# Rounding by integer conversion and a separate stream for W_down in a cross-attention and ternary-FFN kernel

## The chip, the cores and the metric

The kernel runs on one core of one Trainium2 chip. Times are device microseconds of one execution of the program; the profile counts in microseconds from the first instruction of the profiled execution.

## The reference

There are 32 blocks of x and of the context, each 128 by 512 in f32. The first half is a cross-attention that treats the 128 rows as channels and the 512 columns as time; the second half is a feed-forward part with 8-bit activations and ternary weights. Cut to what matters:

```python
# x, ctx: (32, 128, 512); Wq, Wk, Wv, Wo: (128, 128); w_gate, w_up: (2048, 512); w_down: (512, 2048)
def xattn(x, c):                                  # 8 heads of 16 channels, rotary on the first 8
    q, k, v = Wq @ x + bq, Wk @ c + bk, Wv @ c + bv
    q, k = rope(q), rope(k)
    p = softmax(q.T @ k / 4)                      # 512 x 512 for each head
    return Wo @ (p @ v) + bo

def act_quant(x):                                 # per row
    scale = 128 / clip(max(abs(x)), 1e-5)
    return clip(round(x * scale), -128, 127) / scale

def weight_quant(w):                              # one scale for the matrix
    scale = 1 / clip(mean(abs(w)), 1e-5)
    return clip(round(w * scale), -1, 1) / scale

def ffn(x):
    g = act_quant(x) @ weight_quant(w_gate).T
    u = act_quant(x) @ weight_quant(w_up).T
    h = fwht(silu(g) * u)                         # normalized Walsh-Hadamard transform over 2048
    return act_quant(h) @ weight_quant(w_down).T

x = x + xattn(layernorm(x), ctx)
x = x + ffn(layernorm(x))
```

## The kernel before

**One stream per step.** The body of the program is some forty Python generators, one for each step of the work (`s_load`, `s_a`, ... `s_dn`), each looping over the 32 blocks (or 64 half blocks of four heads). A step yields what it needs next: an engine with an estimated duration, a buffer from a ring (`get`, given back with `p.put`), or a mark that another step sets (`on`, set with `p.mark`). The class `Plan` runs all of them against an estimated clock while the program is built, and so fixes the order of every engine's instructions, and of the DMAs on the SyncE queue (SP), which issues all DMAs. Among the steps that could start within a small window on an engine, `rank` prefers the lowest number: a constant for the step from `CFG`, plus `T` times the block, less a bonus (`stick`) for a matmul in the mode that TensorE is in. If a step names several engines, the first is preferred by `pen` microseconds, except in the last blocks. An operation that is marked `port` is planned so that VectorE's does not overlap one of GpSimd (POOL). The engines then run their instructions in that order, each waiting on semaphores.

**Attention.** `s_load` brings x and context; `s_a`, `s_a2` and `s_a3` do the layer norm, the q and k projections and the rotary part (four operations on POOL, L575 to L585) and write the result to DRAM (`xd`); `s_st` reads it back in the layout for scores. `s_mpe` computes scores only to find their row maxima on VectorE (L642, L657; `pS` is a single buffer of two banks), `s_epe` computes them again transposed with the maximum subtracted (L712, `pT`, single too), `s_eact` takes the exponential on ScalarE (L725), `s_eav` multiplies with v (L746). Score matmuls use 48 or 50 rows of the array, the v product 32 columns. `s_o` divides, projects and adds x.

**FFN.** `s_o2` normalizes, scales and rounds a block's rows to integers in bf16 (`xq`) and transposes them by DMA (L864). `s_gpe` and `s_upe` are the gate and up matmuls (L880). `s_bf` does the first four of the Hadamard's steps as adds and subtracts on POOL (L964), `s_zt` to `s_yv` the rest by transposes and matmuls. `s_am` finds the row maximum, `s_q` multiplies by the scale (L1099, POOL), `s_q1` and `s_q2` round and clip on ScalarE, and `s_dn` does the 16 down matmuls (L1141), multiplies and adds the residual on VectorE (L1147), and stores.

**Rounding.** Adding 12582912 (`MAGIC`) to an f32 number leaves its nearest integer in the low bits. x is rounded so into a PSUM buffer (L854) and brought back by VectorE (L857). y is rounded in place (L1109); L1123 then writes `relu(MAGIC + 127 - y)`, that is 127 minus the clipped integer, in bf16. So the down product has the wrong sign and an offset of 127 times W_down's column sums. One more matmul per block (L1142, two rows: `NEG` times `CS`) takes the offset out, and the sign goes into the factor `yc` (L1090).

**Weights.** W_gate, W_up and W_down (4 MB each) come as twelve pieces of 128 by 2048 into the buffers that z and y use later: `s_w` loads (L354), `s_w1` sums absolute values on ScalarE (L367) and makes the scale, `s_w2` scales and adds MAGIC (L391, ScalarE first), `s_w3` clips (L401, VectorE first), `s_w4` subtracts MAGIC into the fp8 weights (L409, ScalarE), and at the end sums W_down's columns for `CS` (L418, 16 matmuls, four small VectorE operations and a DMA). Block 0's gate matmuls wait for all three matrices:

```python
            if b == 0:
                yield "on", "wr", 2
```

Of the kernel before, what the change touches and what calls it, by code (L numbers as in the profile page):

```python
# [13 lines left out]
F8 = mybir.dt.float8e4  # L14
AF = mybir.ActivationFunctionType
# [5 lines left out]
MAGIC = 12582912.0  # L21
# [4 lines left out]
    "a": 17040.0,  # L26
    "a2": 9587.6,
    "a3": 24145.2,
    "am": 15370.4,
    "bf": 32443.0,  # L30
    "const": -13702.6,
    "dn": -12954.6,
    "eact": -26357.5,
    "eav": 10024.8,
    "epe": -25661.6,
    "gact": 12255.9,
    "gpe": 25689.6,
    "hi": 17693.4,
    "hm": -13331.7,
    "init": -13147.7,  # L40
    "lo": 14260.1,
    "load": -14103.3,
    "mdve": -26910.2,
    "mfin": -15116.6,
    "mpe": -17532.8,
    "o": -16894.5,
    "o2": -35355.2,
    "q": 9579.7,
    "q1": 31393.3,
    "q2": 30321.2,  # L50
    "st": -39068.5,
    "u": 12892.7,
    "udve": -12899.7,
    "upe": 40468.8,
    "v": 41001.5,
    "w": 11036.2,
    "w1": 23901.9,
    "w2": 38371.3,
    "w3": 34207.9,
    "w4": 33907.2,  # L60
    "yv": -12466.7,
    "zt": 12210.4,
    "T": 69.4,
    "eps": 0.025,
    "pen": 8.4,
    "stick": 7462.1,
    "epspe": 0.214,
# [5 lines left out]
    "xq": 1, "xqT": 2, "pf": 3, "z0": 2, "z1": 1, "hl": 2, "y": 1, "yq": 2, "ot": 1,  # L73
# [3 lines left out]
class Plan:  # L77

# [16 lines left out]
    def __init__(self, nc, rings, cfg):  # L95
# [12 lines left out]
        self.locked = False  # L108
        self.tail = 0
# [11 lines left out]
    def step(self, t):  # L121
        self.now = max(t[1], t[7] + self.LAT[t[6]]) if t[6] else t[1]
        while True:
            now = self.now
            r = next(t[3], None)
            if self.now != now:
                t[1] = self.now
            t[2] = r
            if r is None:
                self.tasks.remove(t)  # L130
                return
            if r[0] != "at":
                return
            t[0] = self.cfg[t[4]] + self.cfg["T"] * r[1]
            t[5] = r[1]
# [44 lines left out]
    def run(self):  # L180
        for t in list(self.tasks):
            self.step(t)
        while True:
# [4 lines left out]
            for t in self.tasks:  # L188
# [5 lines left out]
                elif isinstance(r[0], tuple):  # L194
                    f = [(self.start(t, e), e, d) for e, d in zip(*r[:2])]
                    pen = self.cfg["pen"] if t[5] < self.tail else 0.0
# [29 lines left out]
def xattn_ffn(  # L226
# [37 lines left out]
    MAG = const.tile([128, 1], F32, name="MAG")  # L264
    nc.vector.memset(MAG, MAGIC)
    NMAG = const.tile([128, 1], F32, name="NMAG")
    nc.vector.memset(NMAG, -MAGIC)
    MAG7 = const.tile([128, 1], F32, name="MAG7")
    nc.vector.memset(MAG7, MAGIC + 127.0)
# [10 lines left out]
    CW = const.tile([128, 388], F32, name="CW")  # L280
    WQ, WK, WVT, BRP, MASK = CW[:, 0:128], CW[:, 128:256], CW[:, 256:384], CW[:, 384:386], CW[:, 386:387]
    NEGC = CW[:, 387:388]
# [14 lines left out]
    ob = const.tile([128, 1], BF, name="ob")  # L297
    nc.vector.memset(ob, 1.0)
    NEG = const.tile([2, 128], BF, name="NEG")
    CS = const.tile([2, 512], BF, name="CS")  # L300

    p = Plan(nc, RINGS, CFG)
    p.tail = NB - 2
# [22 lines left out]
    def s_init():  # L326
        yield "on", "cw"
        yield "dve", 0.2
        nc.vector.tensor_scalar(NEG, ones[0:2, :], NEGC[0:2], None, ALU.mult)
# [15 lines left out]
    WR = ("z0", "z1", "z0", "y")  # L345

    def s_w():
        for n in range(12):
            m, k = divmod(n, 4)
            src = srcs[m][0][k]  # L350
            yield "get", WR[n % 4]
            yield "dma", 2.9
            w = fp.tile([128, 2048], F32, name=WR[n % 4], bufs=2 if WR[n % 4] == "z0" else 1)
            nc.sync.dma_start(out=w.rearrange("p (j i) -> p j i", j=4) if m == 2 else w, in_=src)  # L354
            WT[n] = w
            p.marks["w", n] = p.done
            p.now = p.done - 2.9

    def s_w1():
        for m in range(3):  # L360
            for n in range(4 * m, 4 * m + 4):
                yield "on", "w", n
                for h in range(2):
                    yield ("act", "dve"), (1.1, 1.13)
                    w, a = WT[n][:, bass.ts(h, 1024)], acc[:, 2 * n + h : 2 * n + h + 1]
                    if p.eng == "act":
                        nc.scalar.activation(AB, w, AF.Abs, accum_out=a)  # L367
                    else:
                        nc.vector.tensor_reduce(a, w, AX.X, ALU.add, apply_absolute_value=True)
            yield "get", "pf"  # L370
            yield "pe", 0.1
            pw = ps_f.tile([128, 512], F32, name="pf")
            nc.tensor.matmul(pw[:, 0:8], ones, acc[:, 8 * m : 8 * m + 8], start=True, stop=True)
            yield "dve", 0.1
            sw = SW[:, m : m + 1]
            nc.vector.tensor_reduce(sw, pw[:, 0:8], AX.X, ALU.add)
            p.put("pf")
            yield "dve", 0.1
            nc.vector.tensor_scalar(sw, sw, 1.0 / (NI * 128 * 512), EPS, ALU.mult, ALU.max)
            yield "dve", 0.1  # L380
            nc.vector.reciprocal(SC[:, m : m + 1], sw)
            p.mark("sw", m)

    def s_w2():
        for n in range(12):
            m = n // 4
            yield "on", "sw", m
            yield ("act", "pool", "dve"), (1.95, 2.7, 1.25), "port"
            w = WT[n]
            if p.eng == "act":  # L390
                nc.scalar.activation(w, w, AF.Identity, bias=MAG, scale=SC[:, m : m + 1])  # L391
# [826 lines left out]
```

## Time and profile before

| | |
|---|---|
| median of 3 runs | 1450.17 us (1441.77 to 1455.94) |
| the profiled execution | 1449.79 us |
| its span, mean granted TensorE clock | 1447.9 us, 0.950 |
| TensorE busy (PE) | 1354.9 us, 94% |
| ScalarE (ACT), VectorE (DVE) | 1192.3 us, 82%; 1173.9 us, 81% |
| GpSimd (POOL) | 990.2 us, 68% |
| moved by DMA | 215.23 MB, 149 GB/s |

The span is that of one execution, and the execution's own time is a little longer. "Busy" leaves out waiting, and TensorE's matmuls are pipelined, so that a busy TensorE may still be slow; the granted clock says at which rate it ran. A timeline row gives start, duration, engine, line of the program, operation, output and input by the program's names, and in brackets the idle time before it with what ended it. PEld is the loading of weights into the array, which overlaps the matmuls; SPq is the queue that issues DMAs. The page's slices cut the span into 40 parts of 36 us; a digit is the busy share in tenths.

### The profile page before, as it was taken

Reading aid. Unit: us, or ns where it says so; the run is one execution under the profiler, and the core shown is the slowest. Engines: PE = TensorE matmul, PEld = TensorE weight load, DVE = VectorE, ACT = ScalarE, POOL = GpSimd, SP = SyncE. Lnnn points to the kernel's source line nnn. Section 1 sums busy time; section 2 is a strip of 40 time slices with the busy share of each in tenths; the row PEclk is TensorE's granted clock in tenths of the full one; section 3 lists DMA queues with packets and bytes.
Section 4 is the critical chain, followed back from the end, with each engine's and each line's share of the span. In section 5 each row is a group of like instructions: output and inputs, shape, how many; then the busy total and the mean of one; then the engine's idle time right before and its main releaser. Section 6 shows DMA issues by size and latency. Waiting matters only on the chain.

```text
span 1447.9 us, 21862 instructions
## 1 busy us (share of the span) xinstructions
PE 1354.9 (94%) x7448; PEld 529.9 (37%) x7448; DVE 1173.9 (81%) x1755; ACT 1192.3 (82%) x1575; POOL 990.2 (68%) x778
## 2 busy tenths in 40 slices
PE   3797799999999999999999999999999999999965
PEld 1222233333334343333334433334333434433322
DVE  2975878888888888888888888888889888886565
ACT  5778977888988888888888888888888888888743
POOL 3112319987777878877777787887777777777830
PEclk7567999999999999999999999999999999999986
DMA  8948745454456565555445556555544555321100
GB/s 284 294 145 270 220 110 159 145 145 117 150 157 173 166 175 166 155 151 149 118 153 161 170 170 174 167 153 147 144 129 149 163 170 155 94 72 43 41 26 14
DMA packets 137699, 215.23 MB, mean 149 GB/s; under 512 B 37618, under 2 KB 39924, under 8 KB 136564
## 3 DMA queue, kind: packets, MB, share of 16 engines
q1 hardware_dynamic: 137588, 213.84, 50.4%
q8 instruction: 59, 0.97, 0.3%
q14 instruction: 52, 0.43, 0.1%
HBM read 107.35 MB, written 93.85 MB: 139 GB/s over the span
## 4 chain that ended last, share of the span: by engine, by line
PE 77%; POOL 7%; DVE 6%; ACT 5%; DMA 3%; issue 2%; SPq 0%; POOLq 0%; ACTq 0%; DVEq 0%
PE pav L746 16%; PE pf L880 13%; PE pT L712 13%; PE pS L642 9%; PE pf L1141 8%; POOL z L964 4%; PE pf L472 4%; PE pf L984 4%; PE pf L1023 3%; ACT P L725 2%; PE pf L821 2%; PE pf L552 2%; PE pf L1024 2%; DVE M L657 2%; POOL N L812 1%
## 5 line engine op out<-in xcount | busy, mean ns | idle before, releaser
L964 POOL TENSOR_TENSOR z<-z 128x512 f32<-128x512 f32 x489 | 616.7, 1283 | 103.0 <-DVE z L935 60.7
L657 DVE TENSOR_REDUCE M<-pS 128x2 f32<-128x1024 f32 x488 | 595.1, 1219 | 90.6 <-PE pS L642 89.1
L725 ACT ACTIVATE P<-pT 128x1024 f32<-128x1024 f32 x512 | 523.0, 1022 | 145.6 <-PE pT L712 144.0
L746 PE MATMUL pav<-P,va 128*32 128x512 f32 x2048 | 281.8, 623 | 0.0
L712 PE MATMUL pT<-qs,ks 50*128 50x512 f32 x1024 | 260.1, 504 | 20.8 <-ACT P L725 18.7
L642 PE MATMUL pS<-ks,qs 48*128 48x512 f32 x976 | 227.5, 457 | 12.3 <-DVE M L657 7.5
L712 PEld LDWEIGHTS pT<-qs,ks 50*128 50x128 f32 x1024 | 97.8, 187 | 242.2 <-ACT P L725 144.0
L448 POOL TENSOR_TENSOR arstd<-arstd,MHALF 128x1 f32<-128x1 f32 x32 | 18.5, 579 | 195.6 <-DVE arstd L445 160.5
L880 PEld LDWEIGHTS <-xqT 128*128 128x128 bf16 x1024 | 91.8, 99 | 155.3 <-issue 83.2
L1099 POOL TENSOR_TENSOR y<-y,YB 128x1024 f32<-128x1024 f32 x60 | 140.9, 2369 | 9.0 <-ACT YB L1085 9.0
L1141 PE MATMUL pf<-WDQ,yq 128*128 128x512 fp8e4 x512 | 127.9, 396 | 16.3 <-ACT yq L1123 16.3
L1051 DVE TENSOR_REDUCE ya<-y 128x128 f32<-128x1024 f32 x64 | 127.3, 1989 | 12.9 <-ACT y L1038 12.6
L642 PEld LDWEIGHTS pS<-ks,qs 48*128 48x128 f32 x976 | 95.9, 190 | 112.8 <-issue 43.5
L880 PE MATMUL pf<-WGQ,xqT 128*128 128x512 fp8e4 x512 | 131.4, 382 | 0.9 <-DVE ot L1147 0.5
L880 PE MATMUL pf<-WUQ,xqT 128*128 128x512 fp8e4 x512 | 126.8, 381 | 0.5 <-DVE X L525 0.2
L935 DVE TENSOR_TENSOR z<-z,pf 128x512 f32<-128x512 f32 x128 | 84.3, 675 | 17.2 <-PE pf L880 13.7
L996 ACT CAST hi<-pf 128x512 fp32r<-128x512 f32 x128 | 74.1, 586 | 26.8 <-PE pf L984 26.7
L910 ACT ACTIVATE z<-pf,tk 128x512 f32<-128x512 f32 x128 | 84.1, 684 | 8.0 <-PE pf L880 4.7
L1007 DVE TENSOR_TENSOR lo<-pf,hi 128x512 fp32r<-128x512 f32 x128 | 85.5, 675 | 3.0 <-ACT hi L996 3.0
L1141 PEld LDWEIGHTS <-yq 128*128 128x128 bf16 x512 | 46.7, 101 | 99.3 <-ACT yq L1123 27.4
L984 PE MATMUL pf<-CM,z 128*128 128x128 f32 x512 | 82.2, 285 | 0.8 <-DVE z L964 0.4
L1038 ACT COPY y<-pf 128x512 f32<-128x512 f32 x128 | 71.7, 584 | 9.5 <-PE pf L1024 9.4
(118 smaller groups left out, 1780.0 us busy)
## 6 DMA issues: line engine op xcount, KB each, us to landing
xd<-X SPq DMA_DIRECT2D x128, 512.0 KB
qs<-xd SPq DMA_DIRECT2D x128, 192.0 KB
ks<-xd SPq DMA_DIRECT2D x128, 192.0 KB
ud<-U SPq DMA_DIRECT2D x64, 256.0 KB
xt<-x SPq DMA_DIRECT2D x32, 256.0 KB
ct<-cx SPq DMA_DIRECT2D x32, 256.0 KB
RR<-R SPq DMA_DIRECT2D x64, 128.0 KB
N<-ud SPq DMA_DIRECT2D x32, 256.0 KB
```

The lines of the kernel that those rows point to most:

```text
L642: nc.tensor.matmul(ps[e], qs[w, t, bass.ts(qt, 128)], ks[w, t, :], start=True, stop=True)
L657: nc.vector.tensor_reduce(m, ps[2], AX.X, ALU.max)
L712: nc.tensor.matmul(ps[:, e], ks[w, t, bass.ts(kt, 128)], qs[w, t, :], start=True, stop=True)
L725: nc.scalar.activation(P, TQ[u, n], AF.Exp, scale=0.25)
L746: nc.tensor.matmul(av[32 * h : 32 * h + 32, :], va[:, kt, 4 * hf + h, :], P[:, e], start=(kt == 0), stop=(kt == 3),)
L880: nc.tensor.matmul(ps, xqT[:, k, :], W[:, k, bass.ts(c, 512)], start=(k == 0), stop=(k == 3))
L964: E[p.eng].tensor_tensor(ix(dv, k), ix(av, 0), ix(av, 1), o)
L984: nc.tensor.transpose(ps[:, i, :], st[b]["z"][:, bass.ts(4 * c + i, 128)], EYE)
L1007: nc.vector.tensor_tensor(t, F.pop(("z", b, c)), F["hi", b, c].bitcast(F32), ALU.subtract)
L1051: nc.vector.tensor_reduce(ya[:, h], s["y"][:, 8 * h : 8 * h + 8].rearrange("p j t -> p t j"), AX.X, ALU.max, apply_absolute_value=True,)
L1099: E[p.eng].tensor_tensor(y, y, st[b]["YB"].to_broadcast([128, 8, 128]), ALU.mult)
L1141: nc.tensor.matmul(ps, s["yq"][:, j, :], WDQ[:, j, :], start=(j == 0), stop=False)
```

## The change

The MAGIC constants, `NEG`, `CS` and the correction matmul go. x and y are rounded by writing them as int16 (`xi`, `yi`) on ScalarE, and VectorE clips at 127 on the way to bf16. W_gate and W_up come as ten pieces (the last quarter of each in two halves, in the two `yq` buffers); a piece is summed as before, scaled into int8 in half of a `yi` buffer (POOL first) and clipped on VectorE straight into the fp8 weights. W_down has a stream of its own, `s_wd`: it starts after the first two half blocks are staged, reads its four quarters through the single y buffer for the sums, then reads them again, scales and clips. Block 0's gate waits for W_gate and W_up only, its first down matmul for W_down, and its second rounding step for W_gate and W_up, whose pieces use `yq`. In `CFG` all priorities, `T` (69.4 to 110.5), `stick` (7462.1 to 12666.4), `pen` (8.4 to 54.5) and both windows are new numbers, and each step has a second and third priority, for the first four blocks (`.h`) and the last four (`.z`). Apart from these numbers and the removed constants:

```diff
+    p.head = 4
+    p.tail = NB - 4        
...
+            part = ".h" if r[1] < self.head else ".z" if r[1] >= self.tail else ""
+            t[0] = self.cfg.get(t[4] + part, self.cfg[t[4]]) + self.cfg["T"] * r[1]
...
+    WP = [(m, k, 0, 2048, r) for m in range(2) for k, r in enumerate(("z0", "z1", "z0"))]
+    WP = [x for m in range(2) for x in WP[3 * m : 3 * m + 3] + [(m, 3, 1024 * h, 1024, "yq") for h in range(2)]]
...
+    def w_scale(w, wi, m):
+        f = w.shape[1] / 2048
+        yield ("pool", "act", "dve"), (2.6 * f + 0.1, 1.85 * f + 0.1, 1.15 * f + 0.1), "port"
+        if p.eng == "act":
+            nc.scalar.activation(wi, w, AF.Identity, scale=SC[:, m : m + 1])
+        else:
+            E[p.eng].tensor_scalar(wi, w, SC[:, m : m + 1], None, ALU.mult)
+
+    def w_clip(wi, o):
+        yield "dve", 1.1 * wi.shape[1] / 2048 + 0.15, "port"
+        nc.vector.tensor_scalar(o, wi, 1.0, -1.0, ALU.min, ALU.max, saturate=False)
...
     def s_w2():
+        yield "get", "yi"
+        yi = fp.tile([128, NI, 128], I16, name="yi", bufs=RINGS["yi"])
+        yi = yi.rearrange("p j t -> p (j t)").bitcast(I8)
+        WI.extend(yi[:, bass.ts(h, 2048)] for h in range(2))
+        p.mark("wi")
+        for n, (m, k, c, w, r) in enumerate(WP):
             yield "on", "sw", m
+            yield "get", "wi"
+            wi = WI.pop(0)
+            yield from w_scale(WT.pop(n), wi[:, 0:w], m)
...
     def s_w3():
+        for n, (m, k, c, w, r) in enumerate(WP):
+            yield "on", "w2", n
+            wi = WT.pop(n)
+            yield from w_clip(wi[:, 0:w], srcs[m][1][:, k, c : c + w])
...
+    def s_wd():
+        yield "on", "st", 1
+        for n in range(8):
+            ph, k = divmod(n, 4)
+            yield "get", "y"
+            yield "dma", 2.9
+            w = fp.tile([128, 2048], F32, name="y", bufs=1)
+            nc.sync.dma_start(out=w.rearrange("p (j i) -> p j i", j=4), in_=srcs[2][0][k])
+            p.now = p.done
+            if ph:
+                yield "on", "wi"
+                yield "get", "wi"
+                wi = WI.pop(0)
+                yield from w_scale(w, wi, 2)
+                p.put("y")
+                yield from w_clip(wi, srcs[2][1][:, k, :])
+                WI.append(wi)
+                p.put("wi")
+            else:
+                yield from abs_sum(w, 16 + 2 * k)
+                p.put("y")
+            if n == 3:
+                yield from scale(2)
+        p.mark("wr", 2)
+        yield "on", "wr", 1
+        p.put("yi")
...
     def s_o2():
-            yield "get", "pf"
-            nc.scalar.activation(w, l2, AF.Identity, bias=MAG, scale=sx)
-            nc.vector.tensor_scalar(xq, w, -MAGIC, 127.0, ALU.add, ALU.min)
+            nc.scalar.activation(xi, l2, AF.Identity, scale=sx)
+            yield "dve", 0.3, "port"
+            nc.vector.tensor_scalar(xq, xi, 127.0, None, ALU.min)
...
     def s_gpe():
             if b == 0:
-                yield "on", "wr", 2
+                yield "on", "wr", 1
...
     def s_q1():
-                nc.scalar.activation(y, y, AF.Identity, bias=MAG)
+                nc.scalar.copy(st[b]["yi"][:, w], st[b]["y"][:, w])
                 p.mark("q1", b, hf)
+            p.put("y")
...
     def s_q2():
+            if b == 0:
+                yield "on", "wr", 1
...
-                nc.scalar.activation(s["yq"][:, w], s["y"][:, w], AF.Relu, bias=MAG7, scale=-1.0)
+                yield "dve", 0.42, "port"
+                nc.vector.tensor_scalar(s["yq"][:, w], s["yi"][:, w], 127.0, None, ALU.min)
...
     def s_dn():
             if b == 0:
-                yield "on", "cs"
+                yield "on", "wr", 2
...
-                    nc.tensor.matmul(ps, s["yq"][:, j, :], WDQ[:, j, :], start=(j == 0), stop=False)
-            nc.tensor.matmul(ps, NEG, CS, start=False, stop=True)
+                    nc.tensor.matmul(ps, s["yq"][:, j, :], WDQ[:, j, :], start=(j == 0), stop=(j == NI - 1))
```

## The prediction

> **What bounds the kernel now.** I read the page's engine totals and its 40 slices first, then the table of busy time by stretch, then the PE's timeline of one repeating block, and last the timelines of the start and the end.
>
> ```profile
> PE 1354.9 (94%) x7448; PEld 529.9 (37%) x7448; DVE 1173.9 (81%) x1755; ACT 1192.3 (82%) x1575; POOL 990.2 (68%) x778
> ...
> PE   3797799999999999999999999999999999999965
> ...
> PEclk7567999999999999999999999999999999999986
> ```
>
> ```profile
> 105.00:155.00 50.00, 40.28 (x212) 13.07 (x208) 31.02 (x44) 45.66 (x58) 11.44 (x11) 0.83 0.84 266
> 155.00:190.00 35.00, 27.02 (x126) 7.91 (x126) 27.15 (x40) 32.16 (x32) 9.27 (x8) 0.85 0.71 191
> 200.00:1300.00 1100.00, 1093.90 (x6277) 431.24 (x6276) 951.00 (x1398) 945.90 (x1271) 869.26 (x680) 1.00 0.52 149
> ```
>
> The columns of the second fence are stretch, length, busy time of PE, weight loads, DVE, ACT and POOL, granted clock, DMA share, GB/s. From 200 to 1300 us PE is busy 1093.9 of 1100 us at clock 1.00: it is the bound, and a block of 128 rows comes every 40.2 us (the same up-matmul group starts at 547.8 and 588.05), so the stretch holds 27.4 blocks. Per block DVE then works 34.7 us, ACT 34.5, POOL 31.7, so DVE has 5.4 us free. The start is another matter. In 105 to 155 us ACT is busy 91%, in 155 to 190 us 92%, and PE, busy time multiplied by granted clock, does 33.4 of 50 and 23.0 of 35 us: 16.6 and 12.0 us are lost. ACT and what waits behind it bound that part. What ends it is seen in three timelines (start, duration, instruction):
>
> ```profile
> 151.41 2.25 SPq L864 DMA_TRANSPOSE xqT<-xq  x1
> ...
> 184.27 2.00 ACT L409 ACTIVATE WDQ<-y,NMAG 128x2048 fp8e4<-128x2048 f32 x1 [0.47 <-DVE y L401]
> ...
> 187.17 1.89 PE L880 MATMUL pf<-WGQ,xqT 128*128 128x512 fp8e4 x4
> ...
> 190.13 3.61 PE L418 MATMUL pf<-WDQ,ob 128*1 128x512 fp8e4 x16
> ```
>
> Block 0's FFN input is transposed by about 154 us and W_up is ready at 137.4 (its last L409), but the first gate matmul runs at 187.2, right after W_down's last piece, because s_gpe waits for all three matrices. After 195 us PE is full.
>
> **The change, part by part.**
>
> **1. Correction matmul removed.** One block's second down group:
>
> ```profile
> 559.42 1.90 PE L1141 MATMUL pf<-WDQ,yq 128*128 128x512 fp8e4 x8
> 561.26 0.39 PE L1142 MATMUL pf<-CS,NEG 2*128 2x512 bf16 x1
> 561.57 0.50 PE L712 MATMUL pT<-qs,ks 50*128 50x512 f32 x2
> ```
>
> The matmul holds PE from 561.26 to 561.57, 0.31 us (its 0.39 overlaps the next). 27.4 x 0.31 = 8.5 us off the bound.
>
> **2. W_down apart, gate no longer waits for it.** With today's times gate could start near 154 instead of 187 us, and the 12.0 us that PE loses in 155 to 190 can be filled with work that is waiting: -12.0. The 16 column-sum matmuls go too, 3.5 us (190.13 to 193.67) while PE is full: -3.5. ACT loses L409 (12 x 2.0 = 24 us) and, as POOL is now first choice for scaling, L391 (12 x 2.08 = 25 us). Sixteen of these 24 pieces, 33 us, lie between 99 and 187 us among the exponentials, which come every 2.4 us there and every 1.6 us where no weight piece stands between (140 to 155 us). I take half of the 16.6 us lost in 105 to 155 us as regained: -8.3; the bounds are 0 (PE then waits for something else) and all 16.6.
>
> Against that stand costs. Reading W_down twice and halving the last gate and up piece make 18 weight DMAs out of 12: 4 MB more, at the 266 to 310 GB/s of the start 13 to 16 us of transfer, where the DMA share is already 0.71 to 0.84. The single buffer y makes a W_down issue wait on SP until the piece before is read; behind it on SP stand the q/k stores, loads and R swaps of the next block. Today's L354 issues waited at most 2.3 us, so eight of them cost 0 to 18 us. POOL's scaling to int8 is not in the trace: a 2048-wide piece lies between four memsets of 512 (0.53 each, 2.1 us) and two products of 1024 (2.37 each, 4.7 us); I take 2.6, nearer the memset since it reads one tensor, 12 pieces 31 us, on a POOL that is busy 47 of the first 200 us. Rope (1.28 x 4 per block) queues behind. The clip from int8 on DVE replaces L401 (12 x 1.22 us) piece for piece; one element per cycle would double it, 14.6 us more on a DVE with 30% free. I book 3 us for all of this, with bounds 0 and +30. W_down's scale and clip are hidden by the time until block 0 needs them: its first down matmul is at 272 us, and four reads, four sums and eight more steps of some 7 us make about 60 us from 42 us on. Without that cover each us late would show in full. The start: -12.0 - 3.5 - 8.3 + 3 = -20.8.
>
> **3. Activation rounding.** Per block ACT loses L1123 (2 x 1.13 = 2.3 us); L1109 and L854 stay as int16 writes, and I let them keep 1.13 and 0.76, since L1123 at bf16 output costs the same 1.13 as L1109 at f32. x's row no longer takes a PSUM buffer. DVE gets two 1024-wide int16 minima and one of 512 in place of L857 (0.68). No int16 row exists. Nearest are the one-tensor f32 operations L333 (1024 wide, 0.74) and L401 (2048 wide, 1.22): 0.47 per 1024 and 0.27 fixed, so 0.74 and 0.50. Half the slope gives 0.50 and 0.39, one element per cycle (L1099 on DVE) 1.22 and 0.68. DVE's own work thus grows by 2 x 0.74 + 0.50 - 0.68 = 1.3 us (0.7 to 2.4). The Trainium skill (VectorE: DVE Perf Modes, "The perf-mode tier table") puts a 16-bit one-tensor operation from SBUF at four elements a cycle, which by its 693 ns for 2048 would make an estimated 0.42 and 0.30; the sum would be +0.5 instead of +1.3. No row here shows it.
>
> These three are also the first operations of the steady part that DVE makes from SBUF to SBUF at more than one element per cycle, and the start shows what that does to POOL:
>
> ```profile
> 32.78 1.23 DVE L401 TENSOR_SCALAR z<-z 128x2048 f32<-128x2048 f32 x1 [2.16 <-ACT z L391]
> 32.94 2.19 POOL L580 TENSOR_TENSOR R<-R,RR 128x512 f32<-128x512 f32 x1
> ```
>
> POOL's 1.28 us operation takes 2.19 and ends 1.1 us after DVE does: it stood still until DVE was through. In the other direction DVE's L964, normally 0.68, has a maximum of 1.76. POOL is busy 79% of the time, so a DVE minimum finds it working nearly always: on average half of a 1.28 us operation, 0.5 us for each of three, 1.6 us per block, at worst the whole operation, 1.28 + 2 x 2.37 = 6.0 us at most (none at best). The skill states this as a rule (SBUF — State Buffer, "SBUF: two separate sides"): the pair of ports is locked for a whole instruction and the other engine blocks entirely; the row agrees, and the rule speaks against moving work here from ACT to DVE. Added to DVE in all 1.3 + 1.6 = 2.9 of the 5.4 us it has free, so the bound stays PE: 0 at the end. POOL's loss, up to 3 x 0.74 = 2.2 us on 31.7, fits too.
>
> **4. The end.** The last block's chain:
>
> ```profile
> 1434.51 2.34 ACT L1109 ACTIVATE y<-y,MAG 128x1024 f32<-128x1024 f32 x2 [1.29 <-DVE y L1099]
> ...
> 1436.76 2.17 ACT L1123 ACTIVATE yq<-y,MAG 128x1024 bf16<-128x1024 f32 x2
> ...
> 1437.94 5.98 PE L1141 MATMUL pf<-WDQ,yq 128*128 128x512 fp8e4 x16 [5.03 <-ACT yq L1123]
> ...
> 1443.86 0.38 PE L1142 MATMUL pf<-CS,NEG 2*128 2x512 bf16 x1
> ```
>
> Today the first half is ready at 1437.9. Then: 1434.51 + 1.15 + 0.74 = 1436.4, and the second half at 1437.6 is hidden behind eight matmuls at half clock. -1.5, and -0.4 for the correction: -1.9.
>
> **5. The order.** All priorities are new, and the first and last four blocks get their own. That can't be read from the trace. In the steady part each stretch of half-array matmuls (pT, pS) costs about 0.2 us of mode change; a block has 18 such stretches where 16 would do. So 0.4 us per block is the most to gain there (11 us in all), six stretches more would lose 1.2 us (33 us). The end loses about 44 us of PE time in its last 98 us, of which the 10.3 us gap in the chain at 1308 us is what an order could win or lose again. I take 0 for both.
>
> **Sum**, against the profiled execution's 1449.8 us (span 1447.9; the runs' median is 1450.2, so nothing is to be shifted): -8.5 - 20.8 - 1.9 = -31.2, **1418 us**.
>
> **The rivals.**
>
> **A. The shared port decides (slower).** A stalled DVE holds the only pS buffer, so a minimum that waits for POOL delays the next score matmul, and a fixed order can't step round it. For: POOL 79% busy, the 2.19 us row, and 2.3 of DVE's 5.4 free us are waits for pS, hence tied to the order. Against: ACT gets 2.3 us looser, and PE has other work queued. If 2.0 us per block pass through to PE, 27.4 x 2.0 = 55: 1418 + 55 = 1473. With 1.15 us per block the kernel is as before (31.2 / 27.4); beyond that, slower.
>
> **B. The start does not get shorter.** DMA share 0.84, the second W_down read, SP queue and POOL's scaling in rope's way take back the 20.8: 1418 + 21 = 1439. For: SP already serves everything, and PE's clock is 0.50 for most of 20 to 105 us, when W_down plays no part. Against: ACT at 92% with 33 us of work gone.
>
> **C. The order gets worse** by six mode changes per block: 1418 + 33 = 1451. For: DVE's new waits break pairs of pT and pS. Against: ACT's relief makes pairs easier to keep.
>
> **How the numbers follow.** Forecast 0.64, A 0.15, B 0.12, C 0.09. About 1% (14.5 us) is what a measurement of this kernel can tell from no change, its three runs spreading by that much. Faster: 0.61 of the forecast's and 0.05 of B's, 0.66. Same: 0.03 + 0.07 + 0.03 of C = 0.13. Slower: 0.15 + 0.06 of C = 0.21. The forecast's own range: all lost time of 105 to 155 us regained (-8) and the full 11 us from the order and 10 at the end give 1389; the costs of the start at +30 instead of 3 give 1445. For 8 in 10 I reach into A: 1386 to 1463.
>
> **What would show it.** Right: no L1142 and L418 rows; first gate matmul near 150 us with W_down's clip after it or unrelated to it; PE still over 99% busy in the middle with blocks every 39.9 us; ACT near 32 us per block; DVE near 37. Wrong: POOL or DVE operations stretched beyond 1.3 and 0.75 us with PE waiting for DVE's M (A); first gate matmul at 180 us or later with PE waiting for DMA or X (B); a block every 41 us with PE full and more, shorter half-array stretches (C). The step I trust least is the 0 for DVE's waits.

## The result, and the profile after

The changed kernel takes **1527.32 us** (median of four runs, 1525.43 to 1529.28), the kernel before 1446.94 us beside it (1441.77 to 1455.94). The ratio is **1.0549**, 95% interval 1.0489 to 1.0608: 5.5% slower. The forecast was 1418 us, and 1527 lies above its range and above every rival.

The engine totals and slices of the page after, then busy time by stretch with the columns of before:

```profile
PE 1359.7 (89%) x7400; PEld 537.9 (35%) x7400; DVE 1220.1 (80%) x1810; ACT 1087.2 (71%) x1483; POOL 1073.4 (70%) x794
...
PE   3468899999999999999999999999999999987765
...
PEclk8559899999999999999999999999999999999987
```

```profile
105.00:155.00 50.00, 42.06 (x246) 14.58 (x246) 39.41 (x60) 36.96 (x49) 20.21 (x12) 0.92 0.71 227
155.00:190.00 35.00, 30.03 (x157) 9.46 (x154) 24.52 (x34) 22.80 (x28) 18.30 (x9) 0.80 0.78 240
200.00:1300.00 1100.00, 1065.54 (x6029) 418.30 (x6028) 945.85 (x1386) 863.46 (x1164) 817.31 (x636) 0.99 0.51 148
```

The work went where step 1 and step 2 said: 48 matmuls fewer, ScalarE 105 us less busy (1192.3 to 1087.2), VectorE 46 us more. But TensorE now idles 34.5 us of the 1100 from 200 on, where it idled 6.1. In 105 to 190 us ScalarE no longer bounds (74% and 65% busy). The first gate matmul did not come earlier, and W_down has nothing to do with it: W_up's last clip is over at 108.3 us, while block 0's own input is only transposed at 181 us.

```profile
181.24 1.32 SPq L953 DMA_TRANSPOSE xqT<-xq  x1
...
189.22 1.90 PE L969 MATMUL pf<-WGQ,xqT 128*128 128x512 fp8e4 x8
```

The down group ends without the correction's two rows, and in the last block the first half of y is ready 1.56 us after its rounding began (1514.53 to 1516.09), where it took 3.4:

```profile
571.03 1.89 PE L1237 MATMUL pf<-WDQ,yq 128*128 128x512 fp8e4 x8
572.86 0.51 PE L733 MATMUL pS<-ks,qs 48*128 48x512 f32 x2
...
1514.53 2.23 ACT L1202 CAST yi<-y 128x1024 int16<-128x1024 f32 x2 [1.29 <-DVE y L1188]
...
1515.67 0.42 DVE L1219 TENSOR_SCALAR yq<-yi 128x1024 bf16<-128x1024 int16 x1
...
1516.14 4.16 PE L1237 MATMUL pf<-WDQ,yq 128*128 128x512 fp8e4 x11 [3.21 <-DVE yq L1219]
```

Blocks came out every 40.2 us before. After, the last operation of six consecutive blocks (residual and output, L1242) stands at these times, 59, 38, 56, 33 and 23 us apart:

```profile
418.91 0.75 DVE L1242 SCALAR_TENSOR_TENSOR ot<-pf,yc,x 128x512 f32<-128x512 f32 x1 [0.61 <-PE pf L1237]
478.37 0.75 DVE L1242 SCALAR_TENSOR_TENSOR ot<-pf,yc,x 128x512 f32<-128x512 f32 x1 [2.05 <-PE pf L1237]
516.59 0.74 DVE L1242 SCALAR_TENSOR_TENSOR ot<-pf,yc,x 128x512 f32<-128x512 f32 x1
572.96 0.75 DVE L1242 SCALAR_TENSOR_TENSOR ot<-pf,yc,x 128x512 f32<-128x512 f32 x1 [1.46 <-PE pf L1237]
606.23 0.74 DVE L1242 SCALAR_TENSOR_TENSOR ot<-pf,yc,x 128x512 f32<-128x512 f32 x1
628.80 0.73 DVE L1242 SCALAR_TENSOR_TENSOR ot<-pf,yc,x 128x512 f32<-128x512 f32 x1
```

**Where the 77.3 us of span went.** Two landmarks of each block make a ledger: the last copy of attention's product (`U`, L769 before, L860 after) and the output. These are the last of each, after and then before:

```profile
1381.84 0.59 ACT L860 COPY U<-pav 128x512 f32<-128x512 f32 x1 [1.78 <-PE pav L837]
...
1521.42 0.75 DVE L1242 SCALAR_TENSOR_TENSOR ot<-pf,yc,x 128x512 f32<-128x512 f32 x1 [4.20 <-PE pf L1237]
```

```profile
1365.30 0.59 ACT L769 COPY U<-pav 128x512 f32<-128x512 f32 x1
...
1444.28 0.75 DVE L1147 SCALAR_TENSOR_TENSOR ot<-pf,yc,x 128x512 f32<-128x512 f32 x1 [8.55 <-PE pf L1142]
```

| stage | before | after | difference |
|---|---|---|---|
| start, to block 4's `U` | 276.0 | 271.7 | -4.4 |
| middle, blocks 4 to 27 | 927.1 | 946.0 | +18.9 |
| blocks 27 to 31 | 162.2 | 164.2 | +2.0 |
| last `U` to last output | 79.0 | 139.6 | +60.6 |

(The store after the last output takes 0.2 us more.) When attention was done, four blocks' FFN had still to come out before, and six do after: the FFN had fallen two blocks behind, and the end ran it with little to fill TensorE. That is the largest entry of the ledger.

The ledger dates the loss by landmarks, though, and work that moves past a landmark moves with it. In the end TensorE is busy 92.1 us where it was busy 51.3: 128 gate and up and 96 down matmuls stand there, and before it was 47 and 64. What is plain loss is idle time. By the same four stages, the store counted with the last, TensorE idles 77.4, 24.4, 12.5 and 51.3 us after, and 53.8, 2.4, 5.5 and 31.3 before: 23.6, 21.9, 7.0 and 20.0 us more, 72.5 in all. So the start, the middle and the end each lose some 20 us, and the first entry of the ledger looks good because less FFN work was done by then (73 gate and up matmuls where it was 96).

### The profile page after: what moved, and what is told of

Its sections match the earlier page's. It is cut to its first block, busy times and chain, and to the rows that moved or that the text cites. A ratio compares the mean times of both kernels' runs of the same rounds, so it can differ in the third digit from the quotient of the medians.

```text
span 1525.2 us, 21778 instructions
## 1 busy us (share of the span) xinstructions
PE 1359.7 (89%) x7400; PEld 537.9 (35%) x7400; DVE 1220.1 (80%) x1810; ACT 1087.2 (71%) x1483; POOL 1073.4 (70%) x794
## 4 chain that ended last, share of the span: by engine, by line
PE 57%; DVE 15%; POOL 8%; ACT 8%; issue 5%; DMA 5%; SPq 1%; POOLq 0%; ACTq 0%; DVEq 0%
PE pav L837 12%; PE pT L803 10%; PE pf L969 10%; PE pS L733 7%; PE pf L1237 6%; DVE M L748 5%; ACT P L816 4%; POOL z L1053 3%; PE pf L563 2%; PE pf L1073 2%; DVE ya L1140 2%; PE pf L1112 2%; PE pf L643 2%; POOL yi L460 2%; PE pf L912 1%
## 5 line engine op out<-in xcount | busy, mean ns | idle before, releaser
L1053 POOL TENSOR_TENSOR z<-z 128x512 f32<-128x512 f32 x491 | 625.7, 1296 | 140.1 <-DVE z L1024 107.8
L803 PE MATMUL pT<-qs,ks 50*128 50x512 f32 x1024 | 256.3, 496 | 28.8 <-ACT P L816 26.2
L733 PE MATMUL pS<-ks,qs 48*128 48x512 f32 x976 | 231.9, 467 | 40.8 <-DVE M L748 26.9
L1188 POOL TENSOR_TENSOR y<-y,YB 128x1024 f32<-128x1024 f32 x60 | 142.0, 2386 | 42.4 <-ACT YB L1174 42.3
L1237 PE MATMUL pf<-WDQ,yq 128*128 128x512 fp8e4 x512 | 131.2, 404 | 27.0 <-DVE yq L1219 26.9
L969 PEld LDWEIGHTS <-xqT 128*128 128x128 bf16 x1024 | 87.0, 98 | 142.0 <-issue 69.7
L1202 ACT CAST yi<-y 128x1024 int16<-128x1024 f32 x64 | 66.6, 1043 | 21.0 <-POOL y L1188 18.0
L1073 PE MATMUL pf<-CM,z 128*128 128x128 f32 x512 | 78.5, 283 | 1.6 <-DVE mT L775 1.4
```

The costliest lines, as they stand in the source:

```text
L733: nc.tensor.matmul(ps[e], qs[w, t, bass.ts(qt, 128)], ks[w, t, :], start=True, stop=True)
L803: nc.tensor.matmul(ps[:, e], ks[w, t, bass.ts(kt, 128)], qs[w, t, :], start=True, stop=True)
L969: nc.tensor.matmul(ps, xqT[:, k, :], W[:, k, bass.ts(c, 512)], start=(k == 0), stop=(k == 3))
L1053: E[p.eng].tensor_tensor(ix(dv, k), ix(av, 0), ix(av, 1), o)
L1073: nc.tensor.transpose(ps[:, i, :], st[b]["z"][:, bass.ts(4 * c + i, 128)], EYE)
L1188: E[p.eng].tensor_tensor(y, y, st[b]["YB"].to_broadcast([128, 8, 128]), ALU.mult)
```

## The experiments

The explanations to be told apart were: the new **order** of instructions; the **shared port** (rival A: VectorE's minima wait for GpSimd); **GpSimd's scaling** at the start; and **W_down's own stream**. All ratios are to the kernel before, run on the same chip.

**1 and 2. Operations and priorities apart.** One kernel has all of the change's operations under the priorities and windows of before:

```diff
 CFG = {      # the numbers of before
...
-            part = ".h" if r[1] < self.head else ".z" if r[1] >= self.tail else ""
-            t[0] = self.cfg.get(t[4] + part, self.cfg[t[4]]) + self.cfg["T"] * r[1]
+            t[0] = self.cfg[t[4]] + self.cfg["T"] * r[1]
```

> All operations of the changed kernel, but the order made with the priorities, T, stick, pen and windows of the kernel before (one set for all blocks; the weight stream for W_down gets a number of its own). Theory 1, the order: the new priorities let the FFN fall two blocks behind the attention, so that the end is 60 us longer; with the old ones most of the 80 us go, 1440 to 1480. Theory 2, the shared port: the three VectorE minima per block stall VectorE and POOL whatever the priorities, about 2.5 us per block, so 1500 or more. Theory 3, POOL's scaling of the weights (5.45 us for a piece where the order reckons with 2.7): the start stays late whatever the priorities, 1490 to 1520.

The other is the kernel before with the changed kernel's priorities, the same edit backwards.

> All operations of the kernel before, but the order made with the new priorities (with those for the first and last four blocks), T, stick, pen and windows. Theory 1: slower than before by about as much as the change was, 1500 to 1560. Theory 2 and theory 3: none of the new operations is there, so 1440 to 1460.

Measured: new operations with old priorities 1522.97 us, 1.0533 (1.0485 to 1.0581); old operations with new priorities 1559.0 us, 1.0784 (1.0726 to 1.0843). Either half alone loses as much as both. The second has none of the changed operations (against the kernel before a single operation changed engine, from VectorE to GpSimd) and is still 7.8% slower, so the operations are not needed for the loss; theory 1's range held. For the first kernel that theory had said 1440 to 1480, and it missed: the old priorities do not bring the time back, and the run did not clear the operations. A list of priorities need not fit other work.

**3. The scaling off GpSimd.** The changed kernel's order, with ScalarE issuing each scaling at the place that the plan had given it:

```diff
-        if p.eng == "act":
-            nc.scalar.activation(wi, w, AF.Identity, scale=SC[:, m : m + 1])
-        else:
-            E[p.eng].tensor_scalar(wi, w, SC[:, m : m + 1], None, ALU.mult)
+        nc.scalar.activation(wi, w, AF.Identity, scale=SC[:, m : m + 1])
```

> The changed kernel with its planned order, but the 14 weight pieces are scaled to int8 on ScalarE (L391 took 2.08 us for a piece) at the place in the order where POOL did it (5.45 to 6.5 us for a piece, 68 us in all). Theory 3: the start gets some 30 to 50 us shorter and the whole 1475 to 1500. Theory 1: the order and with it the FFN's lag stay, so the end is as long as it was; 1505 to 1525. Theory 2: 1520 to 1530, since the minima are left.

Measured 1516.02 us, 1.0486 (1.0429 to 1.0542). GpSimd's busy time in the first 200 us falls from 114.0 to 49.8, block 0's last `U` comes at 111 us in place of 128, the first gate matmul at 177.9 in place of 189.2, and TensorE idles 66.1 us up to block 4's `U` in place of 77.4. All of it is worth 11 us of 80 by the medians and 9 by the ratios, whose intervals just overlap; theory 3's 30 to 50 us are not there.

**4. The minima off VectorE.** The order of the changed kernel again; the three minima per block become plain copies on ScalarE (the clip at 127 is left out), so nothing of them is left on the shared port.

```diff
-            nc.vector.tensor_scalar(xq, xi, 127.0, None, ALU.min)
+            nc.scalar.copy(xq, xi)
...
-                nc.vector.tensor_scalar(s["yq"][:, w], s["yi"][:, w], 127.0, None, ALU.min)
+                nc.scalar.copy(s["yq"][:, w], s["yi"][:, w])
```

> The changed kernel with its planned order, but x's and y's int16 numbers are brought to bf16 by a copy on ScalarE at the place where VectorE took the minimum; the clip at 127 is left out. VectorE then runs nothing from SBUF to SBUF at more than one element per cycle in the middle of the program. Theory 2: the middle returns to 40 us per block and the whole to 1460 to 1490. Theory 1 and 3: ScalarE gets 2.3 us per block more and the order stays, so 1510 to 1540.

Measured 1569.67 us, 1.0849 (1.0793 to 1.0905): 42 us worse than the changed kernel, and 30 above the range of theories 1 and 3. With rival A it should have been better. The run does not price the port by itself, since ScalarE also took on work in the middle of a fixed order; run 7 does, in another order.

**5. An order alone.** The kernel before, all its operations unchanged, with one number of the plan changed by 10 ns, the planned (not the real) duration of the exponential:

```diff
-                yield "act", 0.92, "exp"
+                yield "act", 0.93, "exp"
```

> The kernel before with the same operations and the same priorities; only the duration that the order reckons with for the exponential is 0.93 us in place of 0.92 (the trace shows 1.02 for both). Theory 4, formed after the first four runs: the priorities of the kernel before fit one order for exactly its own operations and estimates, and anything that changes the list of operations or an estimate yields another order, irregular and some 4 to 7% longer; so 1490 to 1550, with blocks at uneven distances. Theory 2 (VectorE's new minima and the port that it shares with POOL): none of them is here, so 1440 to 1450.

Measured 1505.68 us, 1.0392 (1.0353 to 1.0431): **58 us for an order**. Of some 21,800 instructions two also moved from GpSimd to VectorE, and ScalarE loads its function tables twice more (1577 instructions for 1575). The 1100 us from 200 on:

```profile
200.00:1300.00 1100.00, 1078.20 (x6063) 426.69 (x6063) 917.45 (x1353) 922.09 (x1227) 845.28 (x662) 1.00 0.49 146
```

TensorE idles 21.8 us where the kernel before idled 6.1, and does 214 matmuls fewer in the stretch. Outputs come 35 to 51 us apart up to 854 us and then every 41.6 us until 1187. Its end, last `U` to last output, is 79 us as before, so an order can lose in the middle as well as at the end.

**6 to 8. The operations in the order of before.** These three keep the priorities and the planned durations of before, so that the order stays, and change only what is issued. Run 6 leaves the correction matmul out (y's offset stays in the result):

```diff
-                    nc.tensor.matmul(ps, s["yq"][:, j, :], WDQ[:, j, :], start=(j == 0), stop=False)
-            nc.tensor.matmul(ps, NEG, CS, start=False, stop=True)
+                    nc.tensor.matmul(ps, s["yq"][:, j, :], WDQ[:, j, :], start=(j == 0), stop=(j == NI - 1))
```

> The kernel before in its own order, without issuing the correction matmul (the order still reckons with it); y's offset stays in the result. Step 1 of the prediction: 0.31 us less per block in the part that TensorE bounds, 27.4 blocks, and 0.4 at the end: 1434 to 1438. Rival: the next wait takes it up, 1443 to 1447.

Run 7 has the whole rounding of x and y by int16 and VectorE's minima, without the correction; weights are as before.

```diff
-            nc.scalar.activation(w, l2, AF.Identity, bias=MAG, scale=sx)
+            nc.scalar.activation(xi, l2, AF.Identity, scale=sx)
...
-            nc.vector.tensor_scalar(xq, w, -MAGIC, 127.0, ALU.add, ALU.min)
+            nc.vector.tensor_scalar(xq, xi, 127.0, None, ALU.min)
...
-                nc.scalar.activation(y, y, AF.Identity, bias=MAG)
+                nc.scalar.copy(st[b]["yi"][:, 8 * hf : 8 * hf + 8], y)
...
-                nc.scalar.activation(s["yq"][:, w], s["y"][:, w], AF.Relu, bias=MAG7, scale=-1.0)
+                nc.vector.tensor_scalar(s["yq"][:, w], s["yi"][:, w], 127.0, None, ALU.min)
```

> The kernel before in its own order, with the change's rounding of x and y (int16 from ScalarE, minimum on VectorE at the place in the order where ScalarE's last step of it was) and no correction matmul; the weights as before. Theory 4: the operations of the change cost nothing in a good order, so about what the run without the correction gives, less 1.5 at the end: 1430 to 1440. Theory 2: VectorE's minima wait for POOL, which is busy 79%, and pass about 2 us per block on to TensorE: 1480 to 1500.

Run 8 adds the weights by int8 (scaled on ScalarE, clipped by VectorE into fp8, no third ScalarE pass, no column sums); W_down is not apart, and block 0's gate still waits for it.

```diff
-                nc.scalar.activation(w, w, AF.Identity, bias=MAG, scale=SC[:, m : m + 1])
+                nc.scalar.activation(w8(n), w, AF.Identity, scale=SC[:, m : m + 1])
...
-            E[p.eng].tensor_scalar(w, w, MAGIC - 1.0, MAGIC + 1.0, ALU.max, ALU.min)
+            E[p.eng].tensor_scalar(srcs[m][1][:, k, :], W8.pop(n), 1.0, -1.0, ALU.min, ALU.max, saturate=False)
```

> As the run with x and y by int16 in the old order, and the weights by int8 too: scaled on ScalarE at its old place, clipped on VectorE straight into the fp8 weights, so that ScalarE's third pass (12 x 2.0 us), the 16 column-sum matmuls and the four small operations and the DMA behind them are gone; W_down is not apart, and block 0's gate keeps its place behind it. Theory 4 and step 2 of the prediction: ScalarE gets 24 us and TensorE 3.5 us back in the first 190 us; 10 to 20 us under the run with x and y alone. Rival: the start is bound by the clock of TensorE (0.50 for most of 15 to 105 us) and by DMA, not by ScalarE: at most 4 us.

| run | median us | ratio (95% interval) | us |
|---|---|---|---|
| 6, no correction matmul | 1438.13 | 0.9935 (0.991 to 0.996) | -9.1 |
| 7, int16 rounding of x and y as well | 1437.84 | 0.9937 (0.991 to 0.9964) | -9.4 |
| 8, weights by int8 as well | 1433.02 | 0.9901 (0.9869 to 0.9932) | -14.2 |

In an order that fits, the same operations make the kernel faster. Run 8 missed its range, however: it is 4.8 us under run 7, with intervals that overlap, where 10 to 20 were expected and its rival said at most 4. Run 7 settles rival A for this order. Its minima wait for GpSimd nearly always at x (0.81 us median where 0.27 is possible) and seldom at y, as the two tiles show (minimum, median and maximum in ns):

```profile
L1128 DVE TENSOR_SCALAR yq<-yi x64: 404/414/1987, 270.6 to 1429.4; 128x1024 bf16<-128x1024 int16 x64
...
L860 DVE TENSOR_SCALAR xq<-xi x32: 271/812/842, 146.2 to 1385.4; 128x512 bf16<-128x512 int16 x32
```

Yet TensorE stays full, and blocks come every 39.8 us (400 to 1200 us of run 7, columns as above):

```profile
400.00:1200.00 800.00, 799.66 (x4640) 315.38 (x4638) 716.80 (x1082) 660.53 (x903) 648.03 (x503) 1.00 0.55 159
```

VectorE works 36 us of each block there and still hides it. How often the minima wait is itself a matter of order: of the 64 at y, 5 take over 0.5 us in run 7 and 34 in the changed kernel (median 0.57 us, longest 1.92). Added up over all minima, the time above 0.27 and 0.40 us is 19 us in run 7 and 36 in the changed kernel. No run shows how much of that TensorE feels in the changed kernel's order; run 2, which has no such minimum, loses more than the changed kernel.

**9 to 11. The whole change in other orders.** What was left was the full change, W_down's stream and early gate included, in an order that fits it. Runs 9 and 10 have all its operations. ScalarE is first choice for scaling; the middle is planned with the durations of before, wrong as they now are, and with its priorities; `wd`, the new stream, has the number it had in run 1, and for the first four blocks three priorities are new in run 9 (`hi`, `u`, `v`) and six in run 10 (`dn`, `gact`, `mpe`, `o`, `v`, `yv`). So run 9 differs from run 1 by the planned durations and buffers, the scaling's engine and three numbers, and its blocks come out evenly. The core of the edit:

```diff
 CFG = {      # of before; new for "wd" and, with ".h", for some steps of blocks 0 to 3
...
-        yield ("pool", "act", "dve"), (2.6 * f + 0.1, 1.85 * f + 0.1, 1.15 * f + 0.1), "port"
+        yield ("act", "dve", "pool"), (1.85 * f + 0.2, 1.15 * f + 0.1, 4.6 * f + 1.3), "port"
...
-            yield "act", 0.6
+            yield "get", "pf"
+            yield "act", 0.75
...
-                yield "dve", 0.42, "port"
+                yield "act", 1.05
...
-                yield "pe", 1.73
+                yield "pe", 1.73 + 0.22 * g
```

> All of the change's operations (int16 rounding of x and y, int8 weights, no correction matmul, W_down's own stream, block 0's gate behind W_gate and W_up alone), with two things different from the changed kernel: ScalarE instead of GpSimd is first choice for scaling a weight piece, and the order of the middle is the one of the kernel before (its priorities, and planned with its durations); only the priorities of the weight streams and of the first four blocks are chosen anew. Theory (the operations are worth some 14 us and more, and the change lost its time in the order alone): 1420 to 1435 us, blocks every 39.8 us from 400 to 1200, first gate matmul before 180 us. Rival (W_down apart, with its 18 weight transfers, or block 0's gate running ahead of W_down, is what costs): over 1480.

> As the run before, with another choice of the same priorities for the weight streams and the first four blocks: a second order for the same instructions. Theory: within 15 us of the run before, since the steady part is the same, and any difference lies before 300 us. Rival (an order is a matter of luck in the middle too): the two differ by over 30 us.

Run 11 keeps the changed kernel's shorter planned durations, with the scaling as in the first pair of lines above, and all priorities chosen anew from those of before.

> The same operations again, ScalarE first for scaling, but planned with the changed kernel's own shorter durations, and with priorities chosen anew throughout, starting from those of the kernel before. Theory: between the two, 1435 to 1460: a block every 40 to 40.5 us. Rival (the changed kernel's durations, being nearer the truth or further from it, spoil any order): 1490 or more, with blocks at uneven distances as in the changed kernel.

| run | median us | ratio (95% interval) | first gate matmul | middle |
|---|---|---|---|---|
| 9 | 1428.61 | 0.9863 (0.9822 to 0.9903) | 172.7 | every 39.8 to 40.2 us, once 40.9 |
| 10 | **1424.53** | **0.9848** (0.9811 to 0.9886) | 157.7 | every 39.8 us |
| 11 | 1462.5 | 1.0108 (1.0064 to 1.0153) | 161.4 | every 40.8 us |

Run 10 beats both kernels. Its table by stretch, its transposed input and first gate matmul, three outputs, and its last two landmarks:

```profile
105.00:155.00 50.00, 40.82 (x243) 13.39 (x245) 35.23 (x56) 39.07 (x48) 12.99 (x12) 0.93 0.92 284
155.00:190.00 35.00, 30.88 (x168) 10.78 (x167) 26.98 (x39) 26.78 (x32) 24.29 (x21) 0.95 0.72 200
200.00:1300.00 1100.00, 1093.81 (x6286) 432.79 (x6278) 979.56 (x1474) 897.36 (x1224) 871.38 (x675) 1.00 0.52 149
```

```profile
148.69 1.32 SPq L910 DMA_TRANSPOSE xqT<-xq  x1
...
157.72 1.04 PE L926 MATMUL pf<-WGQ,xqT 128*128 128x512 fp8e4 x4
...
502.01 0.75 DVE L1199 SCALAR_TENSOR_TENSOR ot<-pf,yc,x 128x512 f32<-128x512 f32 x1 [0.60 <-PE pf L1194]
541.83 0.75 DVE L1199 SCALAR_TENSOR_TENSOR ot<-pf,yc,x 128x512 f32<-128x512 f32 x1 [0.60 <-PE pf L1194]
581.65 0.75 DVE L1199 SCALAR_TENSOR_TENSOR ot<-pf,yc,x 128x512 f32<-128x512 f32 x1 [0.60 <-PE pf L1194]
...
1338.82 0.59 ACT L814 COPY U<-pav 128x512 f32<-128x512 f32 x1
...
1416.10 0.75 DVE L1199 SCALAR_TENSOR_TENSOR ot<-pf,yc,x 128x512 f32<-128x512 f32 x1 [4.13 <-PE pf L1194]
```

The rival of run 9 (W_down apart costs) falls: both runs have it apart and are far from 1480, although the DMA share rises to 0.92 in 105 to 155 us. That having it apart gains anything over run 8 is not shown: 0.9848 and 0.9863 to 0.9901, with intervals that overlap. The medians of runs 9 and 10 differ by 4 us, and their steady parts are alike, as was expected of them. So the operations are good for some 22 us in the best order tried. Of the changed kernel's 103 us more (1527.3 less 1424.5), about 10 are GpSimd's scaling by run 3; the rest, some 92, is a difference and not a run of its own, and goes to the order, with the waits of the minima that come with it. Run 11's expectation was missed by 2.5 us above, and its 40.8 us per block show that a regular order can still be a worse one.

**What an unfit order does to TensorE.** For TensorE's matmuls between 400 and 1200 us, per block of 231.25 matmuls, the mean of a whole run (232.25 in run 5, which has the correction). A stretch is a row of pT and pS matmuls with no other between, and their time runs from each one's start to the next start, or to its end where a gap follows:

| kernel | us per block | of it idle | pT and pS matmuls | their stretches |
|---|---|---|---|---|
| run 7 | 39.9 | 0.0 | 11.6 us | 18.0 |
| run 10 | 39.9 | 0.0 | 11.6 us | 18.0 |
| run 11 | 40.9 | 0.3 | 12.0 us | 19.9 |
| changed kernel | 41.8 | 1.0 | 12.2 us | 19.2 |
| run 5 | 42.1 | 0.8 | 12.4 us | 19.6 |
| run 1 | 42.4 | 1.4 | 12.6 us | 20.0 |

Every order that loses shows both losses: TensorE idles, and the half-array matmuls come in one or two stretches more and take half a microsecond to one longer. In the waits of the changed kernel from 500 to 1100 us (total, times, longest) no single resource stands out:

```profile
ACT P L816 <- PE pT L803: 67.1, 85, 2.7
...
POOL z L1053 <- DVE z L1024: 55.3, 15, 8.9
DVE M L748 <- PE pS L733: 43.6, 67, 2.1
```

I read this as each engine waiting for another that the list has turned to other work; no run shows it apart. Against run 10, whose instructions are nearly the same, TensorE idles 165.5 us in place of 94.8: 20 of the 71 us more are in the first 200 us, 6 from 200 to 400, 19 from 400 to 1200, 3 to 1300 and 23 after. The other 35 us of the 105 between the two spans are busy time. The longer pT and pS matmuls, about 0.5 us in each of 32 blocks, are some 15 of them; the rest I did not divide further, though the mean granted clock is lower too (0.945, run 10 0.964).

## Why the prediction was wrong, by its own steps

**Step 5, the order, failed.** It read "I take 0 for both", with bounds of -11 to +33 us in the middle and 10 either way at the end. By the landmarks the end alone lost 60.6 us and the middle 18.9; in idle time of TensorE the loss is spread over start, middle and end. The bounds were made from what the trace of before showed, the price of a mode change and one gap in the end, and so they assumed that the new order would be of the same kind: regular, with the FFN the same distance behind attention. Nothing in the profile said so. Run 5 shows how weak that assumption was: 10 ns in one planned duration cost 58 us. The bound should have come from how an order can fail, by the FFN falling behind: from the last `U` to the last output it takes 79.0 us with the four blocks left over before, 113.6 with five in run 1, 139.6 with six in the changed kernel and 165.1 with seven in run 2, so each block more lengthens the end by 25 to 35 us. Two blocks were enough to pass the whole bound of the end six times over.

**Step 1, the correction matmul,** was right: -8.5 predicted, -9.1 measured (run 6).

**Step 2, the start,** was right about W_down's place and hidden by two things. Its 154 us for the first gate matmul came to 157.7 in run 10 and to 189.2 in the changed kernel. There the cause was not W_down but a late block 0, and part of that is a mis-sized term: scaling on GpSimd. I took 2.6 us for a 2048-wide piece, within 2.1 to 4.7. It takes 5.45 to 6.50:

```profile
L460 POOL TENSOR_SCALAR yi<-z,SC x6: 5447/6450/6498, 28.2 to 93.9; 128x2048 int8<-128x2048 f32 x6
L460 POOL TENSOR_SCALAR yi<-yq,SC x4: 3372/3635/3897, 46.6 to 104.2; 128x1024 int8<-128x1024 f32 x4
L460 POOL TENSOR_SCALAR yi<-y,SC x4: 5448/5448/5449, 137.7 to 193.3; 128x2048 int8<-128x2048 f32 x4
```

That is 73 us, not 31, with the rope of the first blocks queued behind. The 3 us booked for "all of this" became the 9 to 11 of run 3, inside the bound of 30. The gains were taken too large: by the prediction's own measure, busy time multiplied by granted clock, run 10 regains 4.5 us in 105 to 155 us and 6.4 in 155 to 190, where 8.3 and 12.0 were said. And run 8, which frees ScalarE of one of the two passes and TensorE of the column sums, gains 4.8 us on run 7, where the terms for both passes and the sums made 11.8.

**Step 3, the minima,** gave 0 for the right reason. The 0.74 us that I took for 1024 elements was too much: 0.40 undisturbed, against bounds of 0.50 to 1.22. The Trainium skill's rate (VectorE: DVE Perf Modes, "The perf-mode tier table"), which the prediction turned into an estimated 0.42, agrees with the 404 ns of run 7. The wait for GpSimd exists (up to 1.99 us), as the row of before showed; the skill's rule on the locked pair of ports (SBUF — State Buffer, "SBUF: two separate sides") agrees with it. The 1.6 us per block said for this wait were 0.6 in run 7 and 1.1 in the changed kernel. Run 7's TensorE does not feel it. I called this the step I trusted least; in an order that fits it was the soundest of the uncertain ones.

**Step 4, the end,** was right as to its own chain: in the changed kernel y's first half is ready 1.56 us after its rounding began, where 3.4 was the time before. From the last `U` to the last output run 10 takes 77.3 us against 79.0, -1.7 where -1.9 was said, but runs 7, 8 and 9, with the same last steps, take 78.2 to 78.6.

**The sum in an order that fits.** The same ledger for run 10 against before: start -17.7 (predicted -20.8), blocks 4 to 27 -8.3 (predicted -8.5 for the whole steady part), blocks 27 to 31 -0.5, end -1.7, store +0.2. The span falls by 28.0 us where the sum said 31.2; the medians fall by 22.2, since the profile of run 10 is of its fastest execution and that of before of one 3 us over the median. In run 9, with the same operations, the start gains 12.0 us and the span 16.7. In a fitting order the terms other than the order thus make 17 to 28 us of the 31. That run 10's start comes so near is in part luck: its two stretches fell short of what was said, and the rest was gained elsewhere, with scaling on ScalarE instead of GpSimd and with new priorities for the first four blocks. TensorE idles there as long as before (54.3 us for 53.8); what is shorter is its busy time, at a granted clock of 0.86 for 0.80.

**The rivals.** A fell in an order that fits (run 7), and the loss does not need it (run 2). B's sign that the gate comes at 180 us or later did appear, but by GpSimd and the order, not by DMA, and its 1439 is far from the result. C named the right place, and its mechanism is there (1.2 stretches more per block, not six), but it is the smaller part of what a bad order does: idle TensorE and an FFN two blocks behind are the larger. The chances also gave two thirds of C to "slower", although its own 1451 us is the time of the kernel before. None of the cases put the price of an order near 92 us. One row was misread without harm: what starts at 547.8 and 588.05 us is a pT group, not an up-matmul group, and the distance of 40.2 us is right.

Still open: which of the new priorities makes the FFN fall behind, why the plan turns irregular, and how much of the loss passes through the waits of the minima. No run took the priorities apart.

## What to carry to other kernels

Where a plan or a list of priorities fixes the order of instructions, a change of operations is also a change of order, and the second can outweigh the first: here some +92 us against -22. Price the operations with the order held still, by keeping the planned durations of before even where they are wrong, and look for a new order only after that. In a forecast, "the order is new" deserves a wide range on the slow side; a regular distance between blocks, and the number of blocks still open when the first half of the work ends, show at a glance whether an order fits.

## What the runs showed of the hardware that I had not expected

- GpSimd multiplies 128 by 2048 f32 by a column into int8 in 5.45 to 6.50 us (the changed kernel); ScalarE does the same in 2.00 us (run 10).
- VectorE's minimum from int16 to bf16 takes 0.40 us for 1024 elements and 0.27 us for 512 where it does not wait (run 7), against 0.74 for the f32 operation of 1024 (L333 of before); its clip of 2048 elements from int8 to fp8 takes 1.22 us, the same as the f32 clip that it replaces.
- ScalarE's rounding write of 1024 f32 elements to int16 takes 1.04 us, where the f32 one with a bias took 1.13.
